# The near part of the first layer: row tiles in the projection, a shorter softplus, half of the doubling done by engines, and the scan's operand in PSUM

## Chip, core and metric

The kernel runs on one core of one Trainium2 chip. Its time is the device time of one launch in microseconds (us); several runs give a median. Beside the times there is one profiled execution, whose span runs from its first instruction to its last.

## What is computed

Two layers of the same kind follow each other, each added to its input x, an image of 64 x 64 tokens with 96 channels. A layer normalises x by groups, projects it to 192 inner channels (and to a gate z), applies a 3 x 3 convolution per channel and SiLU, runs a state-space scan in four directions over the 4096 tokens, normalises the sum of the four, multiplies by SiLU(z) and projects back to 96 channels. The change touches only the scans of the first layer (index 0 in the code). Cut to what matters, with `u` the convolved tokens in one direction:

```python
x_dbl = u @ x_proj_w                      # 6 + 16 + 16 columns
dt, B, C = x_dbl[..., :6], x_dbl[..., 6:22], x_dbl[..., 22:]
dt = softplus(dt @ dt_proj_w + dt_proj_b)
log_dA = einsum('bld,dn->bldn', dt, -exp(A_log))
dB_u = einsum('bld,bln->bldn', dt, B) * u[..., None]
decay = exp(cumsum(log_dA, axis=1))
h = decay * cumsum(dB_u / (decay + 1e-12), axis=1)
y = einsum('bldn,bln->bld', h, C) + u * D_skip
```

The small constant 1e-12 makes the states fade out: where the decay has fallen far below it, h is nothing in single precision. So in each direction only the first tokens count, and how many depends on the decay of the state.

## The kernel before

Five engines work beside each other and are tied by semaphores: TensorE (PE), VectorE (DVE), ScalarE (ACT), GpSimd (POOL) and SyncE (SP, which here only issues DMAs). Every engine takes its own queue strictly in order. Except in the second layer's main loop, a scheduler in the tile framework fixes the order of each queue when the kernel is built, from its own estimate of costs, and it assigns tiles to memory. A tile with a tag and one buffer can be written anew only when all readers of its previous content are done.

The first layer runs `head` (normalisation, projection, convolution), then `near_scans`, then `tail` (normalisation of y, gate, projection); the second runs `head`, `scans`, `tail`. `near_scans` computes the scans over the tokens that count: 192 for the slowest pair of the 16 states (`NEAR`), 64 for the next pair, 32 for the other six. At its end it stores a flag that tells whether the others really count for nothing; every engine reads it and branches. `far_scans`, behind the branch, covers the case in which they do count. It is not entered with these inputs.

Channels lie on partitions. The 192 channels make three tiles of 64 (`T` = 0, 1, 2). A tile of 128 partitions holds the same 64 channels twice: in the upper half for the even states, in the lower half for the odd. `HALF` is the pair of the two halves. The four directions lie side by side in the free dimension, as two pairs `q` of two directions `d` with 192 tokens each: 768 elements in all. The stage goes through these steps (lines of the kernel before):

1. L269 to L292: for each T, six matmuls with `wide` gather the first tokens of the four directions from `u[T]` into a PSUM tile `nu`, on both halves of the partitions; ACT or DVE copies it to `us`. The PSUM tiles carry the tags y, m, y, with one buffer each. A matmul of 32-bit floats runs as two passes, so the profile counts twice as many.
2. L295 to L304: x_proj, six matmuls `npj` from the upper 64 partitions of `us` and of the weights `xw` (both hold the same data in both halves), accumulated over T for each q; ACT copies the half q=0 to `xd` and DVE the half q=1.
3. L307 to L326: the rows of C go to DRAM and come back broadcast over partitions (`cb`); ACT and POOL split B into three bfloat16 parts (`B3`), so that a bfloat16 matmul with `selh` can spread it exactly.
4. L329 to L354: dt_proj, matmuls `npd` into a PSUM tile with tag B, with directions q=0 on the upper half of the partitions and q=1 on the lower; then softplus as max(x, 0) + log(1 + w), w = exp(-|x|), with a correction for what 1 + w rounds off: `t` is (1 + w) - 1, and w - t is added. The result is `v`.
5. L244 and L356 to L364: `v`, its running sum `sums` (a scan with `steady`, which is 0 at the start of each direction and 1 elsewhere) and the product `dus` = v * u hold each direction once. `both` copies each of the three into a tile with all directions on both halves (`dt`, `S`, `du`), by four DMAs each. Those of dt and S stand in ACT's queue, those of du in SP's.
6. L391 to L414: matmuls spread B over partitions into a PSUM tile, again with tag B.
7. Six units: for each T one with the slowest states (768 elements) and one with the others (256 + 6 x 128 = 1024 elements). `operands` computes the decay `na` = exp(-A dt) and the weight `nwt`, a Tanh of the running sum (1 plus it is twice the factor decay / (decay + 1e-12)), both on ACT, and on DVE the product `nb` = B * du. `scan` multiplies weight and product (L457), scans (L458) and lets POOL multiply with C (L463). `add` sums states with matmuls into a PSUM tile `ny` with tag y, and after both units of a T six DVE additions (L501) bring it into y. Between them `reach` computes the flag; its transpose (L388) uses tag m.

The loop that writes the order of these steps out is

```python
for j in range(-1, len(units) + 1):
    for at, step in ((j + 1, operands), (j, scan), (j - 1, add)):
        if 0 <= at < len(units):
            step(at)
    if j == 1:
        reach()
```

Of the kernel before, what the change touches and what calls it, by code (L numbers as in the profile page):

```python
# [8 lines left out]
F32 = mybir.dt.float32  # L9
BF16 = mybir.dt.bfloat16  # L10
AF = mybir.ActivationFunctionType
ALU = mybir.AluOpType
# [31 lines left out]
def two_ss2d_layers(  # L44
# [195 lines left out]
    def both(dst, src, queue=nc.sync):  # L240

        for half in HALF:
            for h in range(2):
                queue.dma_start(out=dst[half, ..., h, :], in_=src[HALF[h]])  # L244

    def near_scans(weights):
# [5 lines left out]
        with ExitStack() as sc:  # L252
# [19 lines left out]
            for T in range(3):  # L272
                ps = pps.tile([128, 2, 512], F32, tag=("y", "m")[T % 2], name=f"nu{T}")
                nc.tensor.matmul(
# [21 lines left out]
            for T in range(3):  # L296
                for q in range(2):
                    nc.tensor.matmul(
                        ps[:, q], xw[0:64, 0, T, :], us[0:64, T, q],
                        start=(T == 0), stop=(T == 2),  # L300
                    )
# [28 lines left out]
            for T in range(3):  # L330
                for h, half in enumerate(HALF):
# [3 lines left out]
                    )  # L335
            w, ln, t, v, dus, sums = (
                once.tile([128, 3, 2 * NEAR], F32, name=f"n{nm}")
                for nm in ("w", "ln", "t", "v", "dus", "sums")
            )
# [4 lines left out]
            am = decays(weights[2])[0]  # L344
            for T in range(3):
                nc.scalar.activation(w[:, T], ps[:, T], AF.Abs)
                nc.vector.tensor_scalar_max(v[:, T], ps[:, T], 0.0)
            nc.scalar.activation(w, w, AF.Exp, scale=-1.0)
# [3 lines left out]
            nc.vector.tensor_sub(w, w, t)  # L352
            nc.vector.tensor_add(v, v, w)
            nc.vector.tensor_add(v, v, ln)  # L354
            table("exp_and_others")
            both(dt, v, nc.scalar)  # L356
            nc.vector.tensor_tensor_scan(
                sums.rearrange("p t w -> p (t w)"), steady.rearrange("p t w -> p (t w)"),
                v.rearrange("p t w -> p (t w)"), 0.0, ALU.mult, ALU.add,
            )  # L360
            both(S, sums, nc.scalar)
            for h, half in enumerate(HALF):
                (nc.gpsimd, nc.vector)[h].tensor_mul(dus[half], v[half], us[half, :, h])
            both(du, dus)  # L364

# [54 lines left out]
            def operands(j):  # L420
                T, ks = units[j]
                long = sum(4 * kinds[i][0] * (kinds[i][2] - kinds[i][1]) for i in ks)
                a, b, wt, h, hc = live[j] = [
                    nb.tile([128, 1024], F32, tag=nm, name=f"n{nm}{j}")[:, 0:long]
                    for nm in ("na", "nb", "nwt", "nh", "nhc")
                ]
                o = 0
                for i in ks:
                    n, m0, m1 = kinds[i]
                    o0 = o  # L430
                    for m in range(m0, m1):
# [13 lines left out]
                        a[:, o0:o].rearrange("p (s w) -> p s w", w=n)[:, :, 0:1], 0.0  # L445
                    )
                    k = m1 - m0
                    nc.vector.tensor_mul(
                        b[:, o0:o].rearrange("p (n d w) -> p n d w", n=k, w=n),
                        B[i].rearrange("p (n d w) -> p n d w", n=k, w=n),  # L450
                        four(du, T)[:, :, 0:n].unsqueeze(1).to_broadcast([128, k, 4, n]),
                    )

            def scan(j):
                T, ks = units[j]
                a, b, wt, h, hc = live[j]
                nc.vector.scalar_tensor_tensor(wt, wt, 1.0, b, ALU.add, ALU.mult)  # L457
                nc.vector.tensor_tensor_scan(h, a, wt, 0.0, ALU.mult, ALU.add)  # L458
                o = 0
                for i in ks:  # L460
                    n, m0, m1 = kinds[i]
                    s = slice(o, o + 4 * n * (m1 - m0))
                    nc.gpsimd.tensor_mul(hc[:, s], h[:, s], cb[i])  # L463
                    o = s.stop

            def add(j):
                T, ks = units[j]
                hc = live.pop(j)[4]
                if ks[0] == 0:
# [871 lines left out]
```

## Time and profile before

| what | us |
|---|---|
| median of 3 runs | 1588.21 |
| lowest, highest | 1581.85, 1592.22 |
| profiled execution, its own time | 1585.94 |
| its span | 1584.1 |
| DVE busy in the span | 1395.5 (88%) |
| ACT, PE, POOL busy | 1191.5, 1216.4, 1092.8 |
| first matmul of x_proj to its last end | 101.34 to 109.38 |
| v complete | 125.26 |
| first Tanh | 142.71 |
| last addition into y of the first layer ends | 190.16 |
| first matmul of the first tail | 193.15 |

A row of the timeline names the start, the length, the engine, the line in the kernel, the operation, the tile written and the tiles read, their shapes, the count, and in brackets how long the engine had been idle and what released it. SPq and ACTq are DMA issues in the queues of SP and ACT: their length is that of issuing, with the waits in between, not that of the transfer. A wait for several semaphores is put down to the one that came last by the profile, so a named releaser can be a neighbour of the true one. Tile numbers are left out. A group of instructions that follow closely on each other is shown as one row, with a count and the length from the first start to the last end. Most of the second layer appears under L653, the line of a helper that records its operations.

### The profile page before, as it was taken

To read this page: it belongs to the slowest core of one execution; us is meant where nothing else is said; L and a number is where in the kernel's file an instruction comes from. 1 tells how busy PE (TensorE), PEld (TensorE's weight loads), DVE (VectorE), ACT (ScalarE), POOL (GpSimd) and SP (SyncE) were. 2 spreads that over 40 slices of the span, in tenths; PEclk is the share of its full clock that TensorE was granted. 3 is DMA by queue.
4 is the path that set the end of the run, shared out by engine and by line. 5 is a ranking of instruction groups with operands and counts; after the bars stand their busy time and mean duration, and the time that the engine had idled before them with its cause. 6 is when DMAs were issued, how large, how long until landed. Compare 5 with 4: busy or idle time off the path is not lost.

```text
span 1584.1 us, 17071 instructions
## 1 busy us (share of the span) xinstructions
PE 1216.4 (77%) x5014; PEld 483.7 (31%) x5014; DVE 1395.5 (88%) x971; ACT 1191.5 (75%) x2448; POOL 1092.8 (69%) x577
## 2 busy tenths in 40 slices
PE   5442687167879888898979887988978898877778
PEld 3121422022323233333323333333333332322223
DVE  6956488935998999999999999999999999999976
ACT  2434135367897998989899989999898989897743
POOL 0022200005988989898989898998989898999760
PEclk8755598556998999999999899999999999999999
DMA  4204052051434362626263543526161626345323
GB/s 108 86 20 97 27 134 91 0 121 28 103 86 111 77 148 62 140 55 134 56 146 82 120 98 90 129 74 148 54 135 55 134 76 139 89 99 125 86 66 109
DMA packets 84307, 148.09 MB, mean 93 GB/s; under 512 B 31676, under 2 KB 35068, under 8 KB 84108
## 3 DMA queue, kind: packets, MB, share of 16 engines
q1 hardware_dynamic: 80428, 143.76, 37.5%
q10 hardware_dynamic: 3776, 3.15, 0.8%
q8 instruction: 41, 0.67, 0.2%
q14 instruction: 62, 0.51, 0.1%
HBM read 80.85 MB, written 12.13 MB: 59 GB/s over the span
## 4 chain that ended last, share of the span: by engine, by line
DVE 32%; issue 21%; PE 13%; ACT 11%; DMA 4%; POOL 4%; SPq 3%; DVEq 0%; ACTq 0%; POOLq 0%
DVE h L653 18%; DVE b L653 7%; PE ys L653 4%; ACT a L653 4%; DVE acc L1121 4%; PE b L653 3%; POOL hc L653 3%; SPq L653 3%; PE pj L653 2%; ACT bT L653 2%; PE pd L653 2%; DMA du<-su 1%; DMA szt<-szd 1%; DVE w L653 1%; DMA cb<-C 1%
## 5 line engine op out<-in xcount | busy, mean ns | idle before, releaser
L653 POOL TENSOR_TENSOR hc<-h,cb 128x1024 f32<-128x1024 f32 x384 | 903.9, 2369 | 222.5 <-DMA dt<-sp 106.8
L653 DVE TENSOR_TENSOR_SCAN h<-a,carry,b 128x1024 f32<-128x1024 f32 x288 | 665.4, 2337 | 30.8 <-PE b L653 10.0
L653 ACT ACTIVATE a<-dt,am 128x1024 f32<-128x1024 f32 x384 | 438.7, 1143 | 95.5 <-DVE h L653 93.8
L653 PE MATMUL ys<-hc,fold 128*64 128x512 f32 x1536 | 435.0, 647 | 2.6 <-POOL hc L653 2.6
L653 ACT ACTIVATE bT<-duT,BT 128x192 f32<-128x192 f32 x1024 | 392.2, 446 | 9.2 <-PE b L653 7.2
L653 PE MATMUL b<-ident,bT 128*128 128x128 f32 x1536 | 222.7, 289 | 31.8 <-DVE h L653 27.5
L653 DVE TENSOR_TENSOR b<-b,du 128x1024 f32<-128x1024 f32 x192 | 232.1, 1209 | 5.3 <-PE b L653 5.3
L653 DVE TENSOR_TENSOR_SCAN h<-a,b 128x1024 f32<-128x1024 f32 x96 | 216.3, 2278 | 21.7 <-PE b L653 15.4
L653 PEld LDWEIGHTS b<-ident,bT 128*128 128x128 f32 x1536 | 176.2, 147 | 159.5 <-DVE h L653 98.1
L653 PE MATMUL b<-B,selh 96*128 96x512 bf16 x384 | 123.2, 404 | 90.2 <-DVE h L653 89.3
L653 PE MATMUL pj<-u,xw 64*124 64x512 f32 x192 | 99.1, 682 | 38.4 <-ACT u L1123 37.7
L653 PEld LDWEIGHTS ys<-hc,fold 128*64 128x64 f32 x1536 | 79.2, 140 | 144.2 <-issue 100.9
L1121 DVE SCALAR_TENSOR_TENSOR acc<-pad,v,acc 128x1052 f32<-128x1052 f32 x96 | 119.1, 1306 | 0.2
L653 PE MATMUL pd<-xd,dwb 29*64 29x512 f32 x192 | 61.6, 703 | 58.2 <-DVE w L653 51.4
L653 PEld LDWEIGHTS <-selh 96*128 96x128 bf16 x384 | 26.3, 99 | 218.7 <-DVE h L653 119.1
L653 POOL TENSOR_TENSOR ln<-ln,w 128x512 f32<-128x512 f32 x45 | 57.6, 1280 | 14.8 <-DVE w L653 14.8
L653 PE MATMUL ys<-y,ident 128*128 128x512 f32 (+1 forms) x120 | 65.3, 651 | 0.0
L653 PEld LDWEIGHTS pj<-u,xw 64*124 64x124 f32 x192 | 34.3, 201 | 99.3 <-issue 43.8
L653 ACT CAST B<-pj 64x512 bf16<-64x512 f32 (+2 forms) x96 | 55.1, 576 | 7.8 <-PE pj L653 7.8
L1123 ACT ACTIVATE u<-acc,v 128x1024 f32<-128x1024 f32 x12 | 13.8, 1146 | 59.3 <-DVE acc L1121 59.3
L653 DVE SCALAR_TENSOR_TENSOR w<-pd,w 128x512 f32<-128x512 f32 x48 | 32.1, 668 | 29.8 <-ACT pd L653 29.2
L653 POOL TENSOR_TENSOR sp<-sp,ln 128x512 f32<-128x512 f32 x45 | 57.6, 1279 | 0.0
(159 smaller groups left out, 1132.7 us busy)
## 6 DMA issues: line engine op xcount, KB each, us to landing
cb<-C SPq DMA_DIRECT2D x256, 256.0 KB, 4.1
dt<-sp SPq DMA_DIRECT2D x192, 128.0 KB, 4.2
du<-su SPq DMA_DIRECT2D x192, 128.0 KB, 4.0
szd<-sz SPq DMA_DIRECT2D x24, 256.0 KB, 2.3
szt<-szd SPq DMA_DIRECT2D x24, 256.0 KB, 8.2
xT<-xs SPq DMA_DIRECT2D x8, 384.0 KB
xs<-xT SPq DMA_DIRECT2D x1, 1536.0 KB
xs<-xT SPq DMA_DIRECT2D x8, 192.0 KB
```

Source lines behind the costliest of these rows:

```text
L653: ins = op(*args, **more)
L1121: nc.vector.scalar_tensor_tensor(acc, src, wk, acc, ALU.mult, ALU.add)
L1123: nc.scalar.activation(u[b][:, cut].rearrange("p (c r w) -> p c r w", c=2, w=HW), room[:, :, :, 0:HW], AF.Silu, bias=v[:, b, V_CB : V_CB + 1],
```

## The change

- The third `nu` tile takes the tag B, in a tile of that tag's size, of which it uses the first two banks.
- x_proj for q=1 reads the lower 64 partitions of `us` and `xw`, for q=0 the upper.
- One Abs over all three T instead of three, and no separate maximum: the addition of `w` takes the maximum from PSUM in the same instruction.
- `dus` is gone. POOL and DVE write the product v * u directly into the half of `du` that lies on their own partitions; ACT copies v and `sums` into their halves of `dt` and `S`. `across` then copies only the other halves, by two DMAs per tile, all in SP's queue.
- The product with B moves from `operands` to `scan` and goes to a PSUM tile with tag m; the multiplication with the weight writes there too, and the scan reads it from there.

```diff
--- before.py
+++ after.py
@@ -270,7 +270,9 @@
             us = once.tile([128, 3, 2, 2 * NEAR], F32, name="nus")
             k = NEAR // HW
             for T in range(3):
-                ps = pps.tile([128, 2, 512], F32, tag=("y", "m")[T % 2], name=f"nu{T}")
+                ps = pps.tile(
+                    [128, 4 if T == 2 else 2, 512], F32, tag="ymB"[T], name=f"nu{T}"
+                )[:, 0:2]
                 nc.tensor.matmul(
                     ps[:, 0, 0:NEAR], wide[0], u[T][:, 0:NEAR], start=True, stop=True
                 )
@@ -296,7 +298,7 @@
             for T in range(3):
                 for q in range(2):
                     nc.tensor.matmul(
-                        ps[:, q], xw[0:64, 0, T, :], us[0:64, T, q],
+                        ps[:, q], xw[HALF[q], 0, T, :], us[HALF[q], T, q],
                         start=(T == 0), stop=(T == 2),
                     )
             xq = xd[0:NC].rearrange("p (q w) -> p q w", q=2)
@@ -333,35 +335,42 @@
                         ps[half, T], dwb[96 : NC + 1, 0, T, half],
                         xd[96 : NC + 1, 2 * NEAR * h : 2 * NEAR * (h + 1)], start=True, stop=True,
                     )
-            w, ln, t, v, dus, sums = (
+            w, ln, t, v, sums = (
                 once.tile([128, 3, 2 * NEAR], F32, name=f"n{nm}")
-                for nm in ("w", "ln", "t", "v", "dus", "sums")
+                for nm in ("w", "ln", "t", "v", "sums")
             )
             dt, du, S = (
                 once.tile([128, 3, 2, 2 * NEAR], F32, name=f"n{nm}") for nm in ("dt", "du", "S")
             )
             load_exp_ln()
             am = decays(weights[2])[0]
-            for T in range(3):
-                nc.scalar.activation(w[:, T], ps[:, T], AF.Abs)
-                nc.vector.tensor_scalar_max(v[:, T], ps[:, T], 0.0)
+            nc.scalar.activation(w, ps, AF.Abs)
             nc.scalar.activation(w, w, AF.Exp, scale=-1.0)
             nc.scalar.activation(t, w, AF.Identity, bias=one)
             nc.scalar.activation(ln, w, AF.Ln, bias=one)
             nc.vector.tensor_scalar_add(t, t, -1.0)
             nc.vector.tensor_sub(w, w, t)
-            nc.vector.tensor_add(v, v, w)
+            nc.vector.scalar_tensor_tensor(v, ps, 0.0, w, ALU.max, ALU.add)
             nc.vector.tensor_add(v, v, ln)
             table("exp_and_others")
-            both(dt, v, nc.scalar)
+
+            def across(t):
+
+                for h in range(2):
+                    nc.sync.dma_start(out=t[HALF[1 - h], :, h, :], in_=t[HALF[h], :, h, :])
+
+            for h, half in enumerate(HALF):
+                (nc.gpsimd, nc.vector)[h].tensor_mul(du[half, :, h], v[half], us[half, :, h])
+                nc.scalar.copy(dt[half, :, h], v[half])
             nc.vector.tensor_tensor_scan(
                 sums.rearrange("p t w -> p (t w)"), steady.rearrange("p t w -> p (t w)"),
                 v.rearrange("p t w -> p (t w)"), 0.0, ALU.mult, ALU.add,
             )
-            both(S, sums, nc.scalar)
             for h, half in enumerate(HALF):
-                (nc.gpsimd, nc.vector)[h].tensor_mul(dus[half], v[half], us[half, :, h])
-            both(du, dus)
+                nc.scalar.copy(S[half, :, h], sums[half])
+            across(dt)
+            across(du)
+            across(S)
 
             def four(t, T):
 
@@ -420,9 +429,9 @@
             def operands(j):
                 T, ks = units[j]
                 long = sum(4 * kinds[i][0] * (kinds[i][2] - kinds[i][1]) for i in ks)
-                a, b, wt, h, hc = live[j] = [
+                a, wt, h, hc = live[j] = [
                     nb.tile([128, 1024], F32, tag=nm, name=f"n{nm}{j}")[:, 0:long]
-                    for nm in ("na", "nb", "nwt", "nh", "nhc")
+                    for nm in ("na", "nwt", "nh", "nhc")
                 ]
                 o = 0
                 for i in ks:
@@ -444,18 +453,26 @@
                     nc.gpsimd.memset(
                         a[:, o0:o].rearrange("p (s w) -> p s w", w=n)[:, :, 0:1], 0.0
                     )
+
+            def scan(j):
+                T, ks = units[j]
+                a, wt, h, hc = live[j]
+
+                b = pps.tile([128, 2, 512], F32, tag="m", name=f"nb{j}")
+                b = b.rearrange("p a w -> p (a w)")
+                o = 0
+                for i in ks:
+                    n, m0, m1 = kinds[i]
                     k = m1 - m0
                     nc.vector.tensor_mul(
-                        b[:, o0:o].rearrange("p (n d w) -> p n d w", n=k, w=n),
+                        b[:, o : o + 4 * n * k].rearrange("p (n d w) -> p n d w", n=k, w=n),
                         B[i].rearrange("p (n d w) -> p n d w", n=k, w=n),
                         four(du, T)[:, :, 0:n].unsqueeze(1).to_broadcast([128, k, 4, n]),
                     )
-
-            def scan(j):
-                T, ks = units[j]
-                a, b, wt, h, hc = live[j]
-                nc.vector.scalar_tensor_tensor(wt, wt, 1.0, b, ALU.add, ALU.mult)
-                nc.vector.tensor_tensor_scan(h, a, wt, 0.0, ALU.mult, ALU.add)
+                    o += 4 * n * k
+                b = b[:, 0:o]
+                nc.vector.scalar_tensor_tensor(b, wt, 1.0, b, ALU.add, ALU.mult)
+                nc.vector.tensor_tensor_scan(h, a, b, 0.0, ALU.mult, ALU.add)
                 o = 0
                 for i in ks:
                     n, m0, m1 = kinds[i]
@@ -465,7 +482,7 @@
 
             def add(j):
                 T, ks = units[j]
-                hc = live.pop(j)[4]
+                hc = live.pop(j)[3]
                 if ks[0] == 0:
                     live["y"] = pps.tile([128, 2, 512], F32, tag="y", name=f"ny{T}")
                 ps = live["y"][:, :, 0 : 2 * NEAR].rearrange("p q (d w) -> p q d w", w=NEAR)
```

In the order that the scheduler makes of it, the first matmul of the third `nu` tile (L276 in the changed kernel) stands ahead of the second halves of the other two. In DVE's queue the product for `du` stands ahead of the running sum, each unit's product directly ahead of its multiplication and scan, the first of the six additions for T=0 ahead of the third unit's scan, and the last unit's products behind the additions for T=1. On ACT all eight decays of the first two units come ahead of the Tanh instructions. On PE the transpose for the flag comes after the first two sums of states. The queues of the second layer and of head and tail keep their instructions and their order.

## Prediction

> **What bounds the kernel now.** I read the busy table by stretches first, to place the changed stage; then the timeline of that stage, for which instruction waits for which; then the page's groups, for prices of forms that the stage does not use yet. The table's columns: stretch, length, busy time of PE, PE weight loads, DVE, ACT, POOL (with counts), granted PE clock, DMA share, GB/s.
>
> ```profile
> 92.00:110.00 18.00, 13.93 (x34) 9.25 (x34) 3.95 (x6) 5.68 (x7) 1.91 (x3) 0.50 0.00 0
> 110.00:126.00 16.00, 6.34 (x21) 2.73 (x21) 9.67 (x14) 8.88 (x11) 8.01 (x7) 0.50 0.28 66
> 126.00:143.00 17.00, 0.00 (x0) 0.00 (x0) 8.14 (x8) 2.21 (x5) 2.15 (x3) 0.50 0.94 208
> 143.00:190.00 47.00, 27.29 (x97) 20.56 (x97) 32.07 (x40) 18.42 (x44) 13.28 (x16) 0.57 0.01 2
> ```
>
> The changed stage runs from about 92 to 193 us, 6% of the span. No engine is full in it: one chain passes from engine to engine, so a link that shrinks moves everything behind it, the later layer too. In order: projection (PE), softplus (ACT, DVE), doubling (DMA share 0.94), scans. The chain itself, from the timeline (start, length, engine, line, out<-in, in brackets the idle time before and who ended it):
>
> ```profile
> 95.05 1.15 ACT L1123 ACTIVATE u<-acc,v 128x1024 f32<-128x1024 f32 x1 [1.59 <-DVE acc L1121]
> 98.11 1.01 PE L274 MATMUL nu<-u,wide 128*128 128x192 f32 x2 [3.13 <-ACT nus L292]
> 101.34 8.04 PE L298 MATMUL npj<-nus,xw 64*124 64x384 f32 x12
> 110.01 4.69 PE L332 MATMUL npd<-nxd,dwb 29*64 29x384 f32 x12 [0.62 <-ACT nxd L303]
> 115.85 0.49 ACT L346 ACTIVATE nw<-npd 128x384 f32<-128x384 f32 x1 [0.62 <-DVE nv L347]
> 125.34 2.60 POOL L363 TENSOR_TENSOR ndus<-nv,nus 64x1152 f32<-64x1152 f32 x1 [6.08 <-DVE nv L354]
> 125.36 5.00 DVE L357 TENSOR_TENSOR_SCAN nsums<-steady,nv 128x1152 f32<-128x1152 f32 x1
> 130.39 6.84 ACTq L244 DMA_DIRECT2D nS<-nsums  x4
> 137.33 1.92 ACT L435 ACTIVATE nna<-ndt,am 128x768 f32<-128x768 f32 x4 [14.95 <-DMA ndu<-ndus]
> 142.71 2.29 ACT L438 ACTIVATE nnwt<-nS,lneps,am 128x768 f32<-128x768 f32 x4 [3.46 <-DMA nS<-nsums]
> 153.22 2.30 DVE L457 SCALAR_TENSOR_TENSOR nnwt<-nnwt,nnb 128x768 f32<-128x768 f32 x1
> 154.76 4.79 PE L477 MATMUL ny<-nnhc,fold 128*128 128x64 f32 x24 [1.06 <-POOL nna L444]
> 159.59 1.95 DVE L501 TENSOR_TENSOR y<-ny,y 64x192 f32<-64x192 f32 x6 [2.21 <-PE ny L477]
> 162.44 1.22 DVE L457 SCALAR_TENSOR_TENSOR nnwt<-nnwt,nnb 128x1024 f32<-128x1024 f32 x1
> 188.21 1.95 DVE L501 TENSOR_TENSOR y<-ny,y 64x192 f32<-64x192 f32 x6 [8.44 <-PE ny L477]
> 207.80 1.96 PE L1196 MATMUL o<-g,op 64*96 64x512 f32 x8
> ```
>
> To see here: PE waits for a buffer (98.11), not for its input, ready at 96.20; `npj` needs 0.65 us a pass while `npd`, in column halves, needs 0.39; ACT stands behind DVE reads of the same PSUM tile (115.85); the last big wait is Tanh for the DMA of S (142.71). L457 takes 2.30 us on 768 elements at 153.22 but 1.22 us on 1024 at 162.44: only the first lies beside a POOL multiply (152.20 to 154.70).
>
> ```profile
> L653 DVE TENSOR_TENSOR b<-b,du 128x1024 f32<-128x1024 f32 x192 | 232.1, 1209 | 5.3 <-PE b L653 5.3
> L653 DVE TENSOR_TENSOR_SCAN h<-a,b 128x1024 f32<-128x1024 f32 x96 | 216.3, 2278 | 21.7 <-PE b L653 15.4
> ```
>
> The later layer already multiplies and scans with b in PSUM: 1209 ns and 2278 ns at 1024, the scan as in SBUF here (2292 ns). So PSUM operands cost no more.
>
> **What the Trainium skill says.** "SBUF — State Buffer", section "SBUF: two separate sides": a DVE instruction with two SBUF inputs, or in a two-port mode, and a POOL instruction that reads SBUF lock each other out for a whole instruction. The trace agrees: beside POOL's 2.60 us the scan L357 took 5.00 us, where 2292 ns at 1024 and 1758 ns at 768 give 2.55 us for 1152; L457 lost 1.4 us at 153.22 (0.94 us free, at 143.96). "TensorEngine Tiling (Array Packing)", "Key Properties": different tiles work in parallel; under "Gotcha 1" row tiles need different PSUM banks, which the two halves of `npj` have. The trace agrees for row tiles: `o`, two row halves, takes 1.96 us for 8 passes, while full-height passes of 512 columns there come every 0.43 us. "TensorE: Matmul & The Clock Gate", "What's actually happening": PE runs at half clock until kept busy; the table shows 0.50, so I keep cold prices.
>
> **The change, link by link** (own time: span 1584.1, run 1585.94 us).
>
> A, projection. The third `nu` tile takes the tag B, so it no longer waits for the copy of the first. The order of instructions built from the changed kernel also moves its first matmul ahead, to before the second halves of u. The other five (2.66 us in the preceding tile, 92.32 to 94.98) start when u is there: 96.25 to 98.91 instead of 101.42, −2.5 us. ACT's copy of that tile (0.80 us) then ends near 99.8, before its passes are due (101.5). `npj` in row halves: 12 passes, staggered in pairs, are 6.5 x 0.64 + about 0.4 drain = 4.6 us against 8.04, as `npd` takes 4.69: −3.4 us. Bounds: −4 to 0. A = −5.9.
>
> B, softplus. Three Abs (114.73 to 117.45) alternating with DVE maxima become one of 1152; from 0.49 us at 384 and 0.79 us at 768 (a PSUM copy) 1.10 us: −1.6. The maximum moves into L353, which reads PSUM once: same length (1.36 us at 1152; the form costs 668 ns at 512 from PSUM). But POOL's splitting of B (111.56 to 119.26) shifts by 5.9 only, so its last cast, until 113.4, meets L351 at 112.4: one of them waits, and so does L352 (due 113.6), +0.5 us. Matmuls for B now wait for L353 to free the tile; they take 2 us and are wanted ten later, nothing. B = −1.1; v is ready 7.0 us earlier.
>
> C, doubling, counted from v (125.26 before). Before: Tanh starts 17.45 later. The 12 DMAs of 288 KB (3.5 MB) kept the DMA engines full, and ACT could not leave its queue until the fourth S issue (137.23). After: six DMAs, 1.8 MB, all on SP, and ACT copies the near halves. DVE's queue is now product for du, then scan. POOL's product (2.60), DVE's (1.36) and the scan (2.5) all read two SBUF tiles, so they go in series: scan ends at 6.5 instead of 5.1. ACT: dt copies 0.1 to 2.4 (two of 1152, from Exp's 1.16 us each), S copies 6.5 to 8.85, then the eight decay Exps (four took 1.92; the rest 0.39 each: 3.5) until 12.4. SP: dt at 1.3 and 2.4, du at 2.7 and 4.0, S at 7.75 and 8.9. SP's queue holds small loads of the next weights ahead of these; they end at 123.35 before, 5.9 earlier now, so they don't block. The last S lands 8.9 + 3.9 = 12.8 (this trace: 4.2 us from issue for dt; 7.6 for S behind full queues). Bounds of Tanh's start: 12.4, where ACT itself ends, to 16.5. C = 12.8 − 17.45 = −4.65.
>
> D, scans, counted from Tanh. Before: last y sum ends at 190.16, 47.45 later. After, the products sit in DVE's queue just ahead of their unit, one PSUM tile m serves all, the flag's transpose uses it too, and the built order puts the first y sum of T=0 ahead of the third scan and the last two products behind T=1's sums. Step by step: L457 1.05 to 2.0, scan to 3.8, products (1.3) to 5.05, L457 (1.22) to 6.3, scan to 8.65 (before 9.41: two lock waits are gone, two products are new). POOL (2.5) to 11.25, PE (4.85) to 16.1. DVE has done the third L457 by 11.6 and idles: y sum 16.15 to 16.5, scan to 18.3, five sums to 19.9, products 21.2, L457 22.4, scan 24.8 (before 23.3). POOL 27.4, PE (5.4) 32.8, sums 34.8, products 36.1, L457 37.3, scan 39.7, POOL from 40.2 to 42.7 (with the 0.48 gap of before), PE 48.1, sums 50.1. D = +2.65; bounds −1 (had DVE not waited) to +21.5 (below).
>
> Sum: −5.9 − 1.1 − 4.65 + 2.65 = −9.0 us: 1585.94 becomes 1577. The median of the runs is 2.3 us above the profiled run, so I forecast 1579 us. The later layer has the same instructions in the same order; I add nothing for it.
>
> **Rivals.**
> 1. The new order of DVE costs nothing (D = −1) and S lands at once (C = −5): −13 us, 1575. For it: each lock wait (0.8, 1.4, 1.4 us) goes. Against it: the built order, with a y sum that needs PE's 24 passes.
> 2. A front gain is missing: row halves don't overlap (−5.6 us, 1583), or S takes 7.6 us to land as before (C = −0.95, −5.3 us, 1583). For it: 7.6 is the only time for S in the trace. Against: `o`, and half the bytes.
> 3. Slower than before, by one mechanism: the single PSUM tile m with products behind it makes units run one after another to their y sum. In series a T costs 0.96 + 0.94 + 1.76 + 1.81 + 2.9 + 1.26 + 1.22 + 2.29 + 2.5 + 5.38 + 1.95 = 23 us, three 69 against 47.45: +21.5, so +10 in all, 1598. It decides once D exceeds 11.6, over half of that. Against it: m is released by the scan, and the built order keeps POOL and PE of a unit beside the next one's DVE work.
>
> **How the numbers follow.** Forecast 0.65, rival 1 0.13, rival 2 0.18, rival 3 0.04. The runs before spread from 1581.85 to 1592.22, and 1% (16 us) is about what can be told from no change. Over 1% faster needs 7 us more than I count: part of rival 1 plus spread, 0.10. Slower by over 1% is a corner of rival 3: 0.03. Within: 0.87. The range of 1571 to 1587 is rivals 1 and 2 with 4 us of spread each.
>
> **What would show it.** Right: third `nu` tile starting near 96.3; `npj` under 5 us; one Abs; Tanh 12 to 13.5 us after v; a DVE gap of about 4.5 us before the third scan; last y sum near 181. Wrong: `npj` near 8 us, S landing more than 5 us after issue, L457 or the scan longer in PSUM than above, or a later layer that changes by more than 3 us.

## The result, and the profile after

| what | before, us | after, us |
|---|---|---|
| median (7 runs each) | 1588.06 | 1574.53 |
| lowest, highest | 1581.85, 1592.22 | 1572.28, 1585.11 |
| profiled execution, its span | 1585.94, 1584.1 | 1582.22, 1580.4 |
| x_proj `npj` starts, lasts | 101.34, 8.04 | 98.82, 2.65 |
| dt_proj `npd` lasts, ends | 4.69, 114.70 | 2.74, 104.85 |
| v complete | 125.26 | 115.83 |
| first Tanh (after v) | 142.71 (17.45) | 127.91 (12.08) |
| last y sum ends (after first Tanh) | 190.16 (47.45) | 178.87 (50.96) |
| first matmul of the first tail | 193.15 | 182.11 |

The ratio of the times is 0.9936, with a 95% interval of 0.9906 to 0.9965: 0.64% faster, between 0.35 and 0.94%. That is 10.2 us of 1588 (5.6 to 14.9), against 9.0 by the sum of the steps. The seven runs of after lie in two clusters, four near 1573 us with a mean granted clock of 0.881 to 0.887 and three near 1583 with 0.875 to 0.879, the profiled one among them, so their median says less than this interval.

The busy table of the kernel after, in the stretches and with the columns that were shown of before:

```profile
92.00:110.00 18.00, 10.64 (x44) 7.22 (x44) 7.51 (x12) 12.85 (x15) 7.98 (x8) 0.69 0.15 33
110.00:126.00 16.00, 1.65 (x9) 1.02 (x9) 12.76 (x7) 7.45 (x9) 5.68 (x5) 0.50 0.51 122
126.00:143.00 17.00, 7.40 (x30) 5.17 (x30) 10.41 (x14) 13.33 (x31) 4.68 (x7) 0.60 0.07 18
143.00:190.00 47.00, 27.41 (x84) 18.60 (x84) 24.38 (x36) 8.07 (x19) 8.77 (x9) 0.59 0.13 39
```

Two things stand out. The granted clock of the first stretch is 0.69 where it was 0.50. And from 126 to 143 us, where the DMA engines had been at 0.94 of their time and ACT had done 2.21 us of work, ACT now does 13.33 us: the scans have moved into the stretch that the doubling used to fill. The chain itself, from the timeline after:

```profile
96.23 1.01 PE L279 MATMUL nu<-u,wide 128*128 128x192 f32 x2 [1.26 <-ACT u L1140]
98.82 2.65 PE L300 MATMUL npj<-nus,xw 64*124 64x384 f32 x12
102.11 2.74 PE L334 MATMUL npd<-nxd,dwb 29*64 29x384 f32 x12 [0.64 <-ACT nxd L305]
105.30 1.13 ACT L347 ACTIVATE nw<-npd 128x1152 f32<-128x1152 f32 x1
108.83 1.63 POOL L327 TENSOR_TENSOR nleft<-nleft,nB 32x768 f32<-32x768 f32 x1
108.95 2.13 DVE L351 TENSOR_SCALAR nt<-nt 128x1152 f32<-128x1152 f32 x1 [1.58 <-ACT nt L349]
115.87 1.35 DVE L363 TENSOR_TENSOR ndu<-nv,nus 64x1152 f32<-64x1152 f32 x1
115.91 3.77 POOL L363 TENSOR_TENSOR ndu<-nv,nus 64x1152 f32<-64x1152 f32 x1 [4.16 <-DVE nv L354]
117.25 4.85 DVE L365 TENSOR_TENSOR_SCAN nsums<-steady,nv 128x1152 f32<-128x1152 f32 x1
123.32 1.76 SPq L360 DMA_DIRECT2D nS<-nS  x2
127.91 3.82 ACT L447 ACTIVATE nnwt<-nS,lneps,am 128x768 f32<-128x768 f32 x8 [0.34 <-ACT nna L444]
127.92 0.33 DVE L388 TENSOR_TENSOR top<-nS,most 128x12 f32<-128x12 f32 x3 [2.56 <-DMA nS<-nS]
133.36 1.23 DVE L474 SCALAR_TENSOR_TENSOR nb<-nnwt,nb 128x1024 f32<-128x1024 f32 x1
144.04 0.35 DVE L518 TENSOR_TENSOR y<-ny,y 64x192 f32<-64x192 f32 x1 [4.19 <-PE ny L494]
160.97 1.95 DVE L518 TENSOR_TENSOR y<-ny,y 64x192 f32<-64x192 f32 x6 [4.19 <-PE ny L494]
176.92 1.95 DVE L518 TENSOR_TENSOR y<-ny,y 64x192 f32<-64x192 f32 x6 [8.44 <-PE ny L494]
```

To see here: PE waits at 96.23 for ACT's u, its input, where before it waited 3.13 us for a buffer; `npj` and `npd` are far shorter than the 4.6 and 4.69 us of the forecast; L351 is held up by POOL's subtraction at 108.83; ACT now stands only 0.34 us before the Tanh, where it stood 3.46, though it is still S that comes last, since DVE's L388, which needs S, is released by its DMA in the same moment; and DVE stands twice for 4.19 us before y sums. The groups of the later layer have kept their times, for instance its scan (line, engine, operation, shapes, count, busy us, mean ns, idle before):

```profile
L670 DVE TENSOR_TENSOR_SCAN h<-a,b 128x1024 f32<-128x1024 f32 x96 | 216.1, 2277 | 20.8 <-PE b L670 14.5
```

The profiled execution of after gained 11.04 us up to the first tail and only 3.7 over the whole span; this is taken up under "The later layer" below.

### The profile page after: what moved, and what is told of

The parts are those of the page before. It is cut to its first block, busy times and chain, and to the rows that moved or that the text cites. A ratio compares the mean times of both kernels' runs of the same rounds, so it can differ in the third digit from the quotient of the medians.

```text
span 1580.4 us, 17070 instructions
## 1 busy us (share of the span) xinstructions
PE 1210.6 (77%) x5014; PEld 481.7 (30%) x5014; DVE 1393.0 (88%) x968; ACT 1195.8 (76%) x2450; POOL 1093.7 (69%) x577
## 4 chain that ended last, share of the span: by engine, by line
DVE 30%; issue 20%; PE 14%; ACT 11%; POOL 5%; DMA 5%; SPq 4%; DVEq 0%; ACTq 0%; POOLq 0%
DVE h L670 16%; DVE b L670 7%; PE ys L670 4%; POOL hc L670 4%; ACT a L670 4%; DVE acc L1138 4%; SPq L670 3%; PE b L670 3%; PE pj L670 3%; ACT bT L670 3%; PE pd L670 2%; DMA cb<-C 2%; DMA du<-su 1%; DMA szt<-szd 1%; DVE w L670 1%
## 5 line engine op out<-in xcount | busy, mean ns | idle before, releaser
L670 PEld LDWEIGHTS b<-ident,bT 128*128 128x128 f32 x1536 | 176.7, 147 | 161.5 <-DVE h L670 99.8
L670 POOL TENSOR_TENSOR su<-sp,u 128x512 f32<-128x512 f32 x45 | 57.6, 1279 | 0.0
```

What stands on the lines that cost most here:

```text
L670: ins = op(*args, **more)
```

## Experiments

All kernels start from the changed one unless said otherwise. The times inside a stage are from one profiled execution each, and the time given first is that execution's own (the kernel before, run beside them, took 1586.8 to 1589.42). The first three ask where the clock comes from, the next three test B and C, the rest D and what can be put together.

**The tag of the third `nu` tile undone** (e1_nu_tags).

```diff
-                ps = pps.tile([128, 4 if T == 2 else 2, 512], F32, tag="ymB"[T], ...)[:, 0:2]
+                ps = pps.tile([128, 2, 512], F32, tag=("y", "m")[T % 2], name=f"nu{T}")
```

> The changed kernel, with the third nu tile back on the tag y. Read in the profile: npj, npd and the time at which v is complete. In the changed kernel npj takes 2.65 us and npd 2.74, where 4.6 and 4.7 were forecast. Theory: PE had been busy without a gap since 92.3 us and ran at full clock there; with the gap back before the third nu tile, npj starts at 101.3 and takes 4.6 us, npd 4.7, and v is complete near 120.2 instead of 115.8. Rival: two row halves take 2.65 us at any clock; then npj 2.65, npd 2.7 and v near 118.3.

Measured: 1574.79 us. Its timeline, and a row of its busy table:

```profile
98.06 1.01 PE L274 MATMUL nu<-u,wide 128*128 128x192 f32 x2 [3.13 <-ACT nus L292]
101.30 3.02 PE L298 MATMUL npj<-nus,xw 64*124 64x384 f32 x12
```

```profile
103.00:104.00 1.00, 1.00 (x8) 0.43 (x6) 0.00 (x0) 0.00 (x0) 0.00 (x0) 1.00 0.00 0
```

The wait of 3.13 us is back and `npj` starts 2.48 us later, v 2.86 us later (118.69): that is what the tag is worth, as forecast (2.5). But `npj` is still short, and the granted clock reaches 1.00 at 103. So the closed gap is not what lets the clock up (and in after too PE had stood for 1.26 us, at 96.23, which the theory overlooks). Nor does the rival hold to the end: `npj` is not short at any clock, as e3 shows below.

**x_proj on one row tile again** (e2_one_row).

```diff
-                        ps[:, q], xw[HALF[q], 0, T, :], us[HALF[q], T, q],
+                        ps[:, q], xw[0:64, 0, T, :], us[0:64, T, q],
```

> The changed kernel, with x_proj read from the upper partitions alone for both q, as before; the nu tag stays B. Theory (full clock and overlap of the halves each bring a part): npj starts at 98.8 and takes 4.0 to 4.6 us (12 passes of about 0.33), npd about 2.7, v near 117.5. Rival (the row halves brought it all): npj 8.0 us, npd 4.7, v near 123.

Measured: 1585.6 us. Timeline, and the busy table in small stretches (same columns as above):

```profile
98.92 8.04 PE L300 MATMUL npj<-nus,xw 64*124 64x384 f32 x12
107.58 4.69 PE L334 MATMUL npd<-nxd,dwb 29*64 29x384 f32 x12 [0.62 <-ACT nxd L305]
```

```profile
101.00:103.00 2.00, 2.00 (x5) 1.06 (x4) 0.00 (x0) 0.00 (x0) 0.00 (x0) 0.50 0.00 0
```

PE is busy without a break through `npj`, and the clock stays at 0.50 through `npj` and `npd`, as the rival said. Both durations are those of before to the hundredth. In the changed kernel the same table reads

```profile
98.00:99.00 1.00, 1.00 (x7) 0.83 (x8) 0.00 (x0) 0.11 (x2) 0.25 (x2) 0.50 0.00 0
99.00:100.00 1.00, 1.00 (x4) 0.58 (x6) 0.00 (x0) 0.72 (x1) 0.00 (x0) 0.62 0.00 0
100.00:101.00 1.00, 1.00 (x10) 0.56 (x6) 0.00 (x0) 0.00 (x0) 0.00 (x0) 1.00 0.00 0
```

so PE is just as busy, and the clock doubles about 1 us into `npj`: ten passes fall into the last stretch, four into the one before. The row halves are what brought the clock.

**Full height, one pass at a time** (e9_full_height): are two tiles needed, or only the rows?

```diff
+            xh = once.tile([128, 3, NC], F32, name="nxh")
+            nc.gpsimd.tensor_scalar_mul(xh, xw[:, 0], 0.5)
...
-                        ps[:, q], xw[HALF[q], 0, T, :], us[HALF[q], T, q],
+                        ps[:, q], xh[:, T, :], us[:, T, q],
```

> The changed kernel with x_proj as one full-height pass at a time: halved weights (one POOL multiplication ahead of the stage) against both halves of us, which hold the same data, so 12 passes of 128 rows and never two tiles at once. Theory (what counts for the clock is how many rows of the array work): the granted clock leaves 0.50 within some 4 us of the first pass, npj lasts 4 to 6.5 us and npd 2.7. Rival (two row tiles side by side are needed): npj 8.0, npd 4.7, clock 0.50 through both, as with one row tile. Either way v is later than in the changed kernel, 117.5 under the theory, 121.5 under the rival.

Measured: 1576.85 us, v at 121.21. Timeline and the stretch in which the clock rises:

```profile
100.27 6.58 PE L302 MATMUL npj<-nus,nxh 128*124 128x384 f32 x12 [0.41 <-POOL steady L267]
107.48 2.74 PE L336 MATMUL npd<-nxd,dwb 29*64 29x384 f32 x12 [0.62 <-ACT nxd L307]
```

```profile
105.00:106.00 1.00, 1.00 (x4) 0.61 (x3) 0.00 (x0) 0.00 (x0) 0.00 (x0) 0.88 0.00 0
```

The rival falls: with 128 rows the clock rises without two tiles side by side. The theory's kind is right, its size is not: `npj` took 6.58 us where 6.5 was the upper end, since the clock came only at 105.2, 5.0 us into x_proj. And v came at 121.21, hardly earlier than in e2 (121.47), where the theory had 117.5, although `npd` ended 2.05 us earlier than there: the lead of PE was lost again on the way to v, which is what the next experiment looks into.

The moment at which the clock rises differs between the kernels with row halves too: `npj` took 2.65, 3.02, 3.32 and 4.21 us in after, e1, e8 and e3. In e3

```profile
98.21 4.21 PE L300 MATMUL npj<-nus,xw 64*124 64x384 f32 x12
```

the clock was still 0.50 at 102 and `npj` over at 102.42, so 4.21 us is its price at half clock: the forecast had 4.6. The mean clock of a stretch tells when a change fell within it: the 0.62 of after's stretch from 99 to 100 us is a rise at 99.8. Two more stretches of after:

```profile
106.00:107.00 1.00, 0.00 (x0) 0.00 (x0) 1.00 (x1) 0.97 (x2) 0.99 (x1) 0.80 0.11 9
137.00:138.00 1.00, 0.53 (x2) 0.24 (x3) 0.52 (x3) 0.98 (x3) 0.94 (x2) 0.84 0.00 0
```

The clock falls at 106.6 and rises at 137.3, and read in the same way it changes again at 140.7, 151.0, 154.4 and 185.1. These seven times are 2, 9, 1, 3, 1 and 9 steps of 3.41 us apart, and the changes of the other traces lie on such a grid as well. Where the grid lies against the kernel differs from one execution to the next, so how much of `npj` and `npd` runs at full clock is in part luck. It can also fall back early. In e8, with PE busy,

```profile
104.06 3.58 PE L334 MATMUL npd<-nxd,dwb 29*64 29x384 f32 x12 [0.64 <-ACT nxd L305]
```

```profile
106.00:107.00 1.00, 1.00 (x4) 0.23 (x1) 0.00 (x0) 0.99 (x2) 1.00 (x1) 0.50 0.11 20
```

it is at 0.50 again from 105.8, and `npd` takes 3.58 us instead of 2.74; e5 and e7 show the same (3.50 and 3.51).

**Softplus with two DVE operations instead of three** (e8_fold).

```diff
-            nc.vector.tensor_scalar_add(t, t, -1.0)
-            nc.vector.tensor_sub(w, w, t)
-            nc.vector.scalar_tensor_tensor(v, ps, 0.0, w, ALU.max, ALU.add)
+            nc.vector.scalar_tensor_tensor(w, t, -1.0, w, ALU.add, ALU.subtract)
+            nc.vector.scalar_tensor_tensor(v, ps, 0.0, w, ALU.max, ALU.subtract)
```

> The changed kernel, with the two DVE instructions (t - 1, then w minus that) folded into one, (t - 1) - w, which is subtracted in the next. In the changed kernel the first took 2.13 us and the second 1.79, beside POOL's splitting of B. Theory (lock): the single instruction still meets POOL's last cast; v is complete 0.3 to 1.2 us earlier than at 115.8. Rival (no lock, only instruction length): 1.5 us earlier.

Measured: 1580.97 us. Timeline:

```profile
112.47 1.36 DVE L351 SCALAR_TENSOR_TENSOR nw<-nt,nw 128x1152 f32<-128x1152 f32 x1 [3.15 <-ACT nln L350]
112.49 2.02 POOL L328 CAST nB<-nleft 32x768 bf16<-32x768 f32 x1
```

v itself came at 116.69, later than in after, since this execution reached the third `nu` tile 1.28 us later (97.51) and had the slow `npd`; so it is counted from the end of ACT's Ln: v takes 4.25 us from there instead of 5.77. DVE starts 0.02 us ahead of POOL and does its 1.36 us undisturbed; POOL's cast, 1.23 us in after, takes 2.02. The gain has the rival's size (1.5) but not its reason: before, with three operations and L351 free of POOL, the same way took 4.18 us, so what the fold removes is the waiting. L351, one addition over 1152 elements, took 0.76 us before and in e2, where it comes late enough to miss POOL's subtraction, but 2.13 us in after and e9, where it meets it, and L352 behind it 1.79 instead of 1.36. That is most of the lead which e9 lost.

**The doubling by DMA alone again** (e3_all_dma).

```diff
+            both(dt, v, nc.scalar)
...
+            both(S, sums, nc.scalar)
             for h, half in enumerate(HALF):
-                nc.scalar.copy(S[half, :, h], sums[half])
-            across(dt)
-            across(du)
-            across(S)
+                (nc.gpsimd, nc.vector)[h].tensor_mul(dus[half], v[half], us[half, :, h])
+            both(du, dus)
```

> The changed kernel, with the doubling of before: v, its sum and the product once per direction, twelve DMAs, those of dt and S in ACT's queue. From v to the first Tanh the kernel before took 17.45 us and the changed one 12.1. Theory (bytes and ACT's queue): 17 to 17.5 us again. Rival (the gain came with an earlier start and free DMA queues, the halves matter little): 12 to 14 us.

Measured: 1580.34 us. Timeline:

```profile
116.89 5.00 DVE L358 TENSOR_TENSOR_SCAN nsums<-steady,nv 128x1152 f32<-128x1152 f32 x1
134.72 1.52 ACT L439 ACTIVATE nnwt<-nS,lneps,am 128x768 f32<-128x768 f32 x2 [3.72 <-DMA nS<-nsums]
```

The old picture returns: 17.94 us from v to Tanh, a scan of 5.00 us, and ACT waiting 3.72 us for S, as the kernel before did for 3.46. The new doubling is worth 5.9 us as a whole; what the halved bytes, the engines' copies and the move to SP's queue bring each was not separated.

**The ones of the running sum in PSUM** (e6_steady): a scan that reads one SBUF operand, three scans of 384 ahead of DVE's half of the product.

```diff
+            steady = pps.tile([128, 2, 512], F32, tag="y", name="steady")[:, 0, 0 : 2 * NEAR]
...
+            for T in range(3):
+                tc.keep_in_program_order(nc.vector.tensor_tensor_scan(
+                    sums[:, T], steady, v[:, T], 0.0, ALU.mult, ALU.add
+                ))
```

> The changed kernel, with steady in PSUM (384 elements, one scan per T instead of one over all) and the scans ahead of DVE's product, so that no DVE instruction with two SBUF inputs stands beside POOL's product. Theory (the lock holds the running sum and with it S): from v to the first Tanh 9 us instead of 12.1, POOL's product 2.6 us instead of 3.77. Rival (ACT's copies and Exps set it, or a scan from PSUM is slow): 11.5 to 12.5 us.

Measured: 1573.27 us. Timeline:

```profile
116.99 2.65 DVE L363 TENSOR_TENSOR_SCAN nsums<-steady,nv 128x384 f32<-128x384 f32 x3
117.04 2.61 POOL L367 TENSOR_TENSOR ndu<-nv,nus 64x1152 f32<-64x1152 f32 x1 [4.16 <-DVE nv L354]
127.96 2.29 ACT L449 ACTIVATE nnwt<-nS,lneps,am 128x768 f32<-128x768 f32 x4 [1.90 <-DMA nS<-nS]
```

Scan and POOL's product now run side by side at their free lengths (in after 4.85 and 3.77), and ACT's copies of S end 5.0 us after v instead of 8.6. Yet Tanh gains 1.1 us only, because S stands behind du in SP's queue: ACT has been idle for 1.90 us. The rival's 11.5 to 12.5 was nearer to 11.00 than the theory's 9.

**The product with B back in SBUF and in `operands`** (e4_b_sbuf).

```diff
-                b = pps.tile([128, 2, 512], F32, tag="m", name=f"nb{j}")
...
-                nc.vector.scalar_tensor_tensor(b, wt, 1.0, b, ALU.add, ALU.mult)
-                nc.vector.tensor_tensor_scan(h, a, b, 0.0, ALU.mult, ALU.add)
+                nc.vector.scalar_tensor_tensor(wt, wt, 1.0, b, ALU.add, ALU.mult)
+                nc.vector.tensor_tensor_scan(h, a, wt, 0.0, ALU.mult, ALU.add)
```

> The changed kernel, with the products made in operands and kept in SBUF, weight and scan from SBUF as before. From the first Tanh to the last sum into y the kernel before took 47.45 us and the changed one 50.96. Theory (the placement of products and sums in DVE's queue costs more than the lock waits it saves): 47 to 48.5 us, and the waits of L457 beside POOL come back. Rival (the PSUM operand is a gain, the loss lies elsewhere): 51 us or more.

Measured: 1571.6 us. Timeline:

```profile
132.49 2.21 DVE L466 SCALAR_TENSOR_TENSOR nnwt<-nnwt,nnb 128x1024 f32<-128x1024 f32 x1
138.19 2.29 DVE L466 SCALAR_TENSOR_TENSOR nnwt<-nnwt,nnb 128x768 f32<-128x768 f32 x1
```

The lock waits are back (1.23 and 0.96 us in after), and still the stage is 2.4 us shorter, 48.54 us from Tanh to the last y sum. So this part of the change, as it was made, costs more than the waits that it removes.

**DVE's order written out** (e5_order): products, multiplications, scans and y sums of the six units are kept in the order written, and the sums of a T come after the next unit's scan.

```diff
+            keep = tc.keep_in_program_order
...
+                keep(nc.vector.scalar_tensor_tensor(b, wt, 1.0, b, ALU.add, ALU.mult))
+                keep(nc.vector.tensor_tensor_scan(h, a, b, 0.0, ALU.mult, ALU.add))
...
             for j in range(-1, len(units) + 1):
-                for at, step in ((j + 1, operands), (j, scan), (j - 1, add)):
+                for at, step in ((j + 1, operands), (j, scan)):
                     if 0 <= at < len(units):
                         step(at)
+                if "sum" in live:
+                    bring(*live.pop("sum"))
+                if 0 <= j - 1 < len(units):
+                    add(j - 1)
```

> The changed kernel, with DVE's instructions of the six units kept in a written order: product, weight, scan unit after unit, and the six sums of a T only behind the second scan of the next T. Theory (the wait before the third scan and the products behind the sums are what D lost): from the first Tanh to the last sum 40.7 us by the step sum (50.96 in the changed kernel), no DVE idle gap of 4 us before the third and fifth scan. Rival (PE's sums of states are the pace, each T 8.3 us cold): 46 to 50 us.

Measured: 1564.45 us; 42.70 us from Tanh to the last y sum. Timeline:

```profile
148.68 1.95 DVE L522 TENSOR_TENSOR y<-ny,y 64x192 f32<-64x192 f32 x6
161.74 8.77 PE L495 MATMUL ny<-nnhc,fold 128*128 128x384 f32 x32 [4.96 <-DVE y L522]
170.54 1.95 DVE L522 TENSOR_TENSOR y<-ny,y 64x192 f32<-64x192 f32 x6 [8.95 <-PE ny L495]
```

Both gaps of 4.19 us are gone, and with them 8.26 us of the stage (50.96 to 42.70), nearer to the theory's 40.7 than to the rival's 46. What remains is at the end: the last T's matmuls wait for the one PSUM tile y and then run with PE at clock 0.50.

**The same written order with the product in SBUF** (e11_order_sbuf): what is the PSUM operand worth by itself?

```diff
-                b = pps.tile([128, 2, 512], F32, tag="m", name=f"nb{j}")
-                b = b.rearrange("p a w -> p (a w)")
+                b = nb.tile([128, 1024], F32, tag="nb", name=f"nb{j}")
```

> The kernel with the written order of DVE, only that the product with B, the multiplication with the weight and the scan write and read an SBUF tile instead of the PSUM tile m. It tells what the operand in PSUM is worth by itself once the order is right. Theory: multiplication and scan read two SBUF operands again and wait for POOL's product with C of the unit before, about 1 us in the units where it lies on the chain: from Tanh to the last y sum 45 to 46 us instead of 42.7, multiplications of 2.2 us in some units. Rival: the waits fall into DVE's idle time, 42.7 within 0.5.

Measured: 1561.12 us; 41.44 us from Tanh to the last y sum, below what both had expected. Three rows of its timeline, and for the last 32 passes the busy table of this kernel and then of e5:

```profile
133.78 2.07 DVE L474 SCALAR_TENSOR_TENSOR nb<-nnwt,nb 128x1024 f32<-128x1024 f32 x2
135.78 3.92 DVE L475 TENSOR_TENSOR_SCAN nnh<-nna,nb 128x1024 f32<-128x1024 f32 x2
160.80 6.53 PE L494 MATMUL ny<-nnhc,fold 128*128 128x384 f32 x32 [4.21 <-DVE y L521]
```

```profile
160.80:167.33 6.53, 6.53 (x32) 5.18 (x32) 0.00 (x0) 0.00 (x0) 0.97 (x1) 0.70 0.01 3
```

```profile
161.74:170.51 8.77, 8.77 (x32) 7.36 (x32) 0.00 (x0) 0.00 (x0) 0.97 (x1) 0.50 0.02 4
```

From Tanh to the end of the last scan it is 30.93 us (158.80 - 127.87), in e5 29.95 (159.74 - 129.79). So DVE's chain is 1.0 us longer with the operand in SBUF, less than the 2.3 to 3.3 of the theory; it is hidden by the same 32 passes at clock 0.70 instead of 0.50, worth 2.24 us. But the run does not measure the operand alone, since the built order is not that of e5: two multiplications follow each other here and then two scans, so the third unit's product and multiplication stand ahead of the second unit's scan. Two multiplications over 1024 elements take 1.93 and 1.75 us beside POOL, where 1.23 is the free time; how much of the 1.0 us is the operand's was not separated.

**Order, folded softplus and ones in PSUM together** (e7_best), the edits of e5, e6 and e8.

> The three edits of the runs beside it together: written order of DVE's units, steady in PSUM with scans first, folded softplus. Theory: the gains add up, 10 + 3 + 0.7 us, the last sum of the first layer ends near 165 instead of 178.9, and the median falls by 10 to 14 us below that of the changed kernel, ratio to before 0.983 to 0.988. Rival: PE or the doubling of du becomes the pace, ratio 0.990 to 0.994.

Measured: 1561.9 us, the median of 6 runs (1558.58 to 1569.64), before 1586.81; ratio 0.9847, interval 0.9825 to 0.9870. This is faster than both kernels (the ratio of after was 0.9936), and within the theory's range of ratios. v ends at 116.13, Tanh follows 10.99 us later and the last y sum 40.62 us after that, at 167.74, where the theory had 165.

**S ahead of du in SP's queue** (e10_s_first), from e7_best.

```diff
             across(dt)
-            across(du)
             across(S)
+            across(du)
```

> The kernel that joins order, steady in PSUM and folded softplus, with the two DMAs of S ahead of those of du in SP's queue. There S was issued 1.7 us behind du and Tanh waited 1.9 us for it, 10.99 us after v. Theory: Tanh starts 9.2 us after v, where the Exps end, and du lands 1.7 us later, so the first product ends some 11.5 us after v, just about where the first multiplication with the weight stood (12.05): last y sum 39 us after v + 11, that is 166 to 167 if v ends at 116.1 (before this edit 167.74). Rival: the late du takes it all back, L476 not before 12 us after v and the last y sum within 0.4 us of before, counted from v (51.6).

Measured: 1557.94 us. Timeline:

```profile
123.36 3.81 ACT L449 ACTIVATE nnwt<-nS,lneps,am 128x768 f32<-128x768 f32 x8
125.70 0.97 DVE L469 TENSOR_TENSOR nb<-nB,ndu 128x768 f32<-128x768 f32 x1 [1.97 <-DMA ndu<-ndu]
```

Tanh starts 8.82 us after v, 2.2 us sooner; DVE then waits for du, and L476 starts 12.23 us after v (12.05 in e7_best). The last y sum ends 51.49 us after v, where it was 51.61. The rival is right: the wait has only changed its name.

## Why the prediction was right, and where its steps were off

The forecast was 1579.0 us, the medians give 1574.53; the sum of the steps was -9.0 us and the last y sum came 11.29 us earlier (178.87 instead of 190.16). The end agrees, but partly by luck, because errors of opposite sign met: A gained 3.95 us more than forecast, B and D lost 2.38 more.

| step | forecast | measured |
|---|---|---|
| A, projection (to the end of `npd`) | -5.9 | -9.85 |
| B, softplus | -1.1 | +0.42 |
| C, v to first Tanh | -4.65 | -5.37 |
| D, first Tanh to last y sum | +2.65 | +3.51 |
| sum | -9.0 | -11.29 |

**A** fails in one term: "so I keep cold prices". The 2.5 us of the buffer were right (third `nu` tile at 96.23, forecast 96.25). The copy of `npj` came 7.90 us earlier instead of 5.9, and `npd`, which the forecast left at 4.69, took 2.74. The second 1.95 us are the clock alone; of the first 2.0, e3's 4.21 leaves 1.56 to the clock and 0.4 to an overlap that is better than estimated. The execution was a lucky one: in the ten profiles with row halves `npj` took 2.65 (after) to 4.21 us (e3), `npd` 2.74 to 3.58 (e8). The Trainium skill, "TensorE: Matmul & The Clock Gate", section "What's actually happening", lets the clock up after a window of about 3.4 us with a busy PE, and the windows run on by themselves. The steps of 3.41 us agree; the measurement differs in what counts as busy. In e2 passes on 64 rows fill two whole steps (99.9 to 106.7 us, counted back from its next rise at 157.9) and the clock stays at 0.50, while in e9 passes on all rows, again one at a time, let it up. Not every full step does: in e3 PE was busy from 95.62 us, and the step that ended at 99.1 changed nothing. That part stays open.

**B** fails in the lock. The single Abs took 1.13 us (forecast 1.10), and from the end of `npd` to Exp it became 1.18 us shorter (forecast 1.6), since ACT had other work when the early `npd` ended. From Exp to v it became 1.60 us longer, where 0.5 was put in for POOL's last cast. The forecast had POOL's splitting come 5.9 us earlier and L351 7.6; it was 7.90 and 11.02, because the shorter `npd` brings forward softplus but not POOL. So L351 met one instruction of POOL more, its subtraction at 108.83, which it had missed before:

```profile
119.97 0.76 DVE L351 TENSOR_SCALAR nt<-nt 128x1152 f32<-128x1152 f32 x1 [1.92 <-ACT nt L349]
```

The rule that the prediction drew from the Trainium skill ("SBUF — State Buffer", "SBUF: two separate sides"), one side waiting for the other's whole instruction, is what the traces show (L351 at 2.13 instead of 0.76 us); the time at which the two would meet was wrong.

**C** is right in its mechanism (e3 puts the old doubling at 17.94 us) and nearly in its size. The order of the three that lock each other out was not as written: DVE's product went first, POOL's needed 3.77 us instead of 2.60, and the scan still ended 6.27 us after v (forecast 6.5). S landed last, as forecast: L388 and the Tanh start together at 127.92 and 127.91, 12.08 us after v (forecast 12.8). ACT's Exps ended 11.74 us after v (forecast 12.4), so ACT alone would have allowed the Tanh only 0.3 us sooner.

**D** has the right sign, the right place and roughly the right size: DVE idles 4.19 us before the third scan (forecast 4.5). e5 shows that this is the order and no property of PSUM: with the order put right the stage is 8.26 us shorter. L474 and the scan take in PSUM what the forecast said (0.96 and 1.23; 1.75 and 2.29 us). What the PSUM operand saves by itself is open: 1.0 us of DVE's chain by e11, but with another order in it; the prediction did not separate the two effects either.

**The rivals.** The first (-13 us, 1575) is near the measured median, but not for its reason: it needed D = -1, and D was +3.51. The second, a missing front gain, did not happen. The third, units in series, did not either: the POOL and PE work of a unit lies beside the next one's DVE work in all kernels.

**The later layer.** A change of more than 3 us there was to prove the prediction wrong, and in the profiled executions it was there: from the first matmul of the tail to the end of the span 1390.95 us before, 1398.29 after, which took back 7.3 of the 11.04 us. Nothing points to the change as its cause. The same part, with the same instructions, took from 1386.8 (e10) to 1398.3 us (after) over the thirteen profiles, and kernels that differ from the changed one in one edit of the near part lie at both ends: e1 1387.1, e8 1395.8. In the profile of after, a stretch of lower clock can be seen. First the busy table of after for it, then that of before over the same work:

```profile
481.00:556.00 75.00, 63.39 (x263) 24.16 (x264) 67.56 (x39) 63.81 (x139) 65.47 (x33) 0.89 0.43 99
```

```profile
492.00:567.00 75.00, 64.19 (x279) 23.47 (x278) 72.03 (x41) 67.79 (x147) 67.50 (x34) 0.95 0.41 100
```

PE does 263 matmuls in 75 us instead of 279, at 0.89 against 0.95. That the clock is the cause of the whole 7 us is argued, not shown: e2 and e8, whose later part is nearly as long (1395.3 and 1395.8), have 0.95 in this stretch, and over the whole part the mean clock is 0.91 in before and in after. The sign to look for was badly chosen: 3 us is less than what one profile differs from the next by itself. The ratio over seven runs, 10.2 us, is the better witness, and it agrees with the 11 us of the stage.

## What to carry to other kernels

When a change raises how much of the PE array is used, read the granted clock in stretches of one us, for the passes behind it too: here the row tiles brought 3.8 to 5.4 us on their own matmuls and 1.1 to 1.95 us on the ones after, depending on where the execution met the grid of the clock. An operand moved to PSUM to avoid a lock can be worth no more than the waits on the chain (some 1.0 us here, not measured alone), while moving its producer can cost a stall on an in-order engine (2 x 4.19 us, where the kernel before stood 2.21 and 2.80): look at the order that is built, in every run that claims to keep it, and write it out where it matters. Two transfers that feed the same step are worth reordering only if the one put behind is not wanted at the same time (S and du: 2.2 us gained at Tanh, 0.1 us at the end).

## What the runs showed of the hardware

- The granted clock of PE stayed at 0.50 through 8 us of unbroken passes on 64 rows (before, e2), and went to 1.00 with passes on both row halves, 0.9 to 4.3 us after the first (after, e3), and with passes on 128 rows, 5.0 us after the first (e9). It changed only in steps of 3.41 us, which lie differently in each execution, and it fell back to 0.50 within a series of 29-row passes (e8, at 105.8 us).
- When DVE and POOL want the SBUF lock at the same time, the one whose record starts a few hundredths of a us sooner has it for its whole instruction: DVE at 115.87 against POOL's 115.91 in after (POOL took 3.77 us), DVE at 112.47 against 112.49 in e8, but POOL at 125.34 against DVE's 125.36 before (DVE's scan took 5.00 us).
- A scan with one operand in PSUM and one in SBUF is not locked out by a POOL product on SBUF (e6: 2.65 us for three scans of 384 beside POOL's 2.61).
